# A macaron transformer layer on one core: causal masks moved from TensorE to VectorE and GpSimd, and the attention values issued two steps behind the scores

## The chip, the core and the metric

The kernel runs on one core of one Trainium2 chip, as one launch. The metric is the device time of that launch in microseconds; the kernel before was timed three times and the median counts. The core has five engines that run side by side and wait for each other through semaphores: TensorE (PE in the profile; PEld are its weight loads), VectorE (DVE), ScalarE (ACT), GpSimd (POOL) and SyncE (SP), whose queue issues most of the DMAs. Each engine executes its own instructions strictly in the order in which the program lists them, apart from weight loads that run ahead. Matmuls write to PSUM, which here is divided into eight banks of 128 partitions by 512 fp32 values.

## What is computed

The input is one sequence of 2048 tokens with 512 features. Three half-steps follow each other: a gated feed-forward network, causal self-attention with 16 heads of 32 features, and the same feed-forward network again, each on a layer-normed input and added to the residual.

```python
x = x + 0.5 * ffn(layernorm(x), gate, up, down)      # codes of 4 bits with block scales
x = x + attention(layernorm(x), w_qkv, b_qkv, w_out, b_out)
x = x + 0.5 * ffn(layernorm(x), gate, up, down)

def attention(x, w_qkv, b_qkv, w_out, b_out):
    q, k, v = split_heads(x @ w_qkv.T + b_qkv)        # 16 heads x 2048 x 32
    scores = q @ k.T / sqrt(32)
    scores = scores + triu(-inf, k=1)                 # causal
    return merge_heads(softmax(scores) @ v) @ w_out.T + b_out

def ffn(x, gate, up, down):
    return (gelu_tanh(x @ gate.T) * (x @ up.T)) @ down.T
```

The change touches the attention alone, and in it the causal mask, which affects only the 128x128 blocks on the diagonal of the score matrix: blocks above the diagonal are never computed.

## The kernel before

The whole kernel is written with an order by hand: the engines receive their instructions in the order in which the Python code issues them. Tiles come from pools with a fixed number of buffers; a tile's first writer waits for the last reader of the buffer's previous tile. Two PSUM pools matter: `ps_one` has seven banks and serves almost everything, and `ps_acc` has one bank, for the attention output being accumulated (`av`).

The attention works on eight pairs of heads, `p` = 0 to 7. Every pair is gone through twice:

- `maxima(p)` computes scores with queries on the partitions (tile `pm`, L612), and takes row maxima on VectorE (L629, tile `parts`). At the end of each block of 512 queries `g` (there are four), `finish` negates the maximum (L635, `nmax`), GpSimd splits it into three bf16 pieces (L640 and L643, five small instructions that depend on one another), and three steps later `rows` transposes them on TensorE (L650) and ScalarE copies them into `mrow` (L651).
- `attend(p)` computes the scores with keys on the partitions (tile `ps`): first a matmul with ones that puts minus the row maximum into the bank (L705, called `maxrows`), then keys times queries on top of it (L714). ScalarE exponentiates into an SBUF tile `pt` (L736; three buffers). `values` multiplies `pt` with the values and a block of ones, and so accumulates both the output and the softmax's denominator in `av` (L668).

Both run over the same 40 steps of a pair: for each `g` first 4g steps that lie below the diagonal and are 512 wide, then four diagonal steps of width 512, 384, 256 and 128. The main loop interleaves them: one step of `attend(p)` together with one step of `maxima(p + 1)`. The maxima of pair 0 run alone at the start, and pair 7 has no maxima beside it. One step issues, in this order: `maxrows` and the `pm` matmul for both heads, the `ps` matmuls for both heads, the mask matmuls of both sides, the maxima on VectorE (and `finish`), then the exponentials and `values` of the step before, which `pending` holds. A matmul here has 32 rows of contraction, and the two heads of pair p and the two of pair p+1 lie on the four different quarters of the array.

The mask is added by TensorE: on a diagonal step, `mask` issues eight bf16 matmuls for each side (L622 for `pm`, L726 for `ps`), of 32 rows, which add rows of a mask (`mqk`, `mkq`; -1e30 where a key is later than the query) picked by slices of an identity (`pick`). These three constant tiles are filled at the very start by 48 small DMAs on GpSimd's queue (L84).

Beside that run `fill` pieces, on the diagonal steps of some pairs: projections of q, k and v for later pairs (L540, L557; pairs 0, 2 and 4), and output projections (L579; pairs 3, 5 and 7). Pairs 1 and 6 have none, and the pieces of pairs 0 and 2 all fall on the first two diagonal steps. The wide tile of q and k weights for pair 2 is loaded by a DMA that is issued when pair 2 begins (L535).

When an `av` block is complete, ScalarE copies it (L677, `both`), two DMAs move the denominators to the partitions of the outputs (L682, `den`), and four chunks follow, one a step: a reciprocal on VectorE (L685) and two multiplications on GpSimd (L688). At the end of a pair the last `values` is issued at once, and `run_later(1 << 30)` issues at once the `rows` that are due later.

Of the kernel before, what the change touches and what calls it, by code (L numbers as in the profile page):

```python
# [18 lines left out]
P = 128  # L19
# [3 lines left out]
HD = 32  # L23
# [11 lines left out]
def macaron_kernel(ctx: ExitStack, tc: tile.TileContext, x, packed, scales, wqk, bqk, wv, bv, wo, bo, out):  # L35
# [34 lines left out]

    plain = [identb]
    for nm, step, mult in (("mask_qk", -1, 1), ("mask_kq", 1, -1)):
        m = const.tile([P, P], BF16, tag=nm, name=nm)
        nc.gpsimd.memset(m, 0.0)
        nc.gpsimd.affine_select(
            out=m, in_=m, compare_op=ALU.is_ge, fill=MASKED, base=0, pattern=[[step, P]], channel_multiplier=mult
        )
        plain.append(m)

    pick, mqk, mkq = [const.tile([P, 4, P], BF16, tag=nm, name=nm) for nm in ("pick", "mqk", "mkq")]  # L80
    for t4, src in zip((pick, mqk, mkq), plain):
        for r in range(4):
            for j in range(4):
                nc.gpsimd.dma_start(out=t4[HD * r : HD * r + HD, j, :], in_=src[HD * j : HD * j + HD, :])  # L84

# [403 lines left out]
    def attention(xT, xT_f):  # L489
        with tc.tile_pool(name="aw", bufs=1) as aw, tc.tile_pool(name="qk", bufs=1) as qkp, tc.tile_pool(  # L490
# [95 lines left out]
            def quadrant(p, a):  # L586
                r = 2 * (p % 2) + a
                return slice(HD * r, HD * r + HD)

            later, divisions = [], []  # L590

            def run_later(now):
                while later and later[0][0] <= now:
                    later.pop(0)[1]()

            def maxima(p):
# [5 lines left out]
                for g in range(NB):  # L602
                    parts = an.tile([P, 2, 4, g + 1], F32, tag=f"parts{g}", name=f"parts_{p}_{g}")
                    steps = [(i, kb) for i in range(4) for kb in range(g)] + [(i, g) for i in (3, 2, 1, 0)]
                    for i, kb in steps:
                        n = 512 if kb < g else (i + 1) * P
                        ps = [None, None]

                        def matmuls(a):
                            r = quadrant(p, a)  # L610
                            ps[a] = ps_one.tile([P, 512], F32, tag="one", name=f"pm_{p}_{g}_{i}_{kb}_{a}")
                            nc.tensor.matmul(  # L612
                                ps[a][:, :n], lhsT=q[r, bass.ts(4 * g + i, P)], rhs=k[r, kb * 512 : kb * 512 + n],
                                start=True, stop=(kb < g),
                            )

                        def mask():
                            if kb == g:
                                for j in (3, 2, 1, 0):
                                    for a in range(2):  # L620
                                        r = quadrant(p, a)
                                        nc.tensor.matmul(  # L622
                                            ps[a][:, n - P + HD * j : n], lhsT=pick[r, j, :], rhs=mqk[r, j, HD * j :],
                                            start=False, stop=(j == 0),
                                        )

                        def rest(now):
                            for a in range(2):
                                nc.vector.tensor_reduce(parts[:, a, i, kb : kb + 1], ps[a][:, :n], AX.X, ALU.max)  # L629
                            if i == 0 and kb == g:  # L630
                                finish(now)
# [27 lines left out]
            def attend(p):  # L659
# [5 lines left out]

                def values(g, c, off, pt, av):
                    for a in range(2):
# [7 lines left out]
                    if c == 4 * g + 3:  # L675
# [16 lines left out]

                        divisions.extend([lambda: None] * 2 + [lambda j=j: chunk(j) for j in range(4)])

                pending = None
                for g in range(NB):
                    av = None
                    for c in range(4 * g + 4):
# [13 lines left out]
                        def matmuls(a):  # L712
                            r = quadrant(p, a)
                            nc.tensor.matmul(  # L714
                                ps[a][:, off:],
                                lhsT=k[r, bass.ts(c, P)],
                                rhs=q[r, g * 512 + off : (g + 1) * 512],
                                start=False, stop=(c < 4 * g),
                            )

                        def mask():
                            if c >= 4 * g:
                                for j in range(4):
                                    for a in range(2):
                                        r = quadrant(p, a)
                                        nc.tensor.matmul(  # L726
                                            ps[a][:, off : off + HD * j + HD], lhsT=pick[r, j, :],
                                            rhs=mkq[r, j, : HD * j + HD],
                                            start=False, stop=(j == 3),
                                        )  # L730

                        def rest():
                            nonlocal pending, av
                            pt = pp.tile([P, 2, 512], F32, tag="pt", name=f"pt_{p}_{g}_{c}")
                            for a in range(2):
                                nc.scalar.activation(  # L736
                                    pt[:, a, off:], ps[a][:, off:], AF.Exp, scale=1.0 / math.sqrt(HD)
                                )
                            if pending is not None:
                                values(*pending)  # L740
                            if c == 0:
                                av = ps_acc.tile([P, 512], F32, tag="acc", name=f"av_{p}_{g}")
                            pending = (g, c, off, pt, av)

                        yield maxrows, matmuls, mask, rest, c >= 4 * g
                values(*pending)

# [12 lines left out]

            def after_step(diagonal, fill):

                nonlocal now
                now += 1
                run_later(now)
                if divisions:
                    divisions.pop(0)()
                if diagonal:
                    for _ in range(-(-len(fill[0]) // fill[1])):
                        fill[0].pop(0)()  # L770
                    fill[1] -= 1
# [21 lines left out]
            assert not fill  # L793
            run_later(1 << 30)
            plan = {
# [6 lines left out]
            for p in range(NPAIR):  # L802
# [18 lines left out]
                ahead = maxima(p + 1) if p + 1 < NPAIR else iter(())  # L821
                for n, (maxrows, matmuls, mask, rest, diagonal) in enumerate(attend(p)):
                    if n in STARTS:
# [10 lines left out]
                    if other:  # L834
                        other[1]()
                    mask()
                    if other:
                        other[2](now)
                    rest()
                    after_step(diagonal, fill)  # L840
                    for step in extra.get(n, ()):
                        step()
                run_later(1 << 30)
            while divisions:
                divisions.pop(0)()
            for piece in o3[12:]:
# [79 lines left out]
```

## The time and the profile before

| Kernel before | us |
|---|---|
| median of three runs | 3375.31 (3374.28 to 3377.02) |
| the profiled execution, its own time | 3374.09 |
| its span in the profile | 3372.3 |

The three stages, by windows of the trace (busy time of each engine in us, and the mean clock granted to TensorE as a share of full speed):

| Stage | window | PE | DVE | ACT | POOL | clock |
|---|---|---|---|---|---|---|
| first feed-forward | 0 to 1225 | 1178.60 | 922.26 | 214.69 | 661.82 | 0.99 |
| pair 0's maxima and the projections they need | 1225 to 1327 | 100.91 | 54.03 | 17.69 | 7.03 | 0.98 |
| pairs 0 to 7 | 1327 to 2180 | 836.1 | 492.9 | 358.7 | 161.7 | 0.97 to 1.00 |
| second feed-forward | 2180 to 3372 | 1167.87 | 598.48 | 203.51 | 303.30 | 0.99 |

(The third row adds up eight windows, cut at 1430, 1530, 1630, 1738, 1875, 1970 and 2070.) The cuts lie near the beginnings of pairs 1 to 7. The device time of the profiled execution is 1.8 us more than its span. A busy TensorE means that a matmul was in the array, not that all of it was in use: most matmuls in the attention occupy a quarter or a half of the array and run side by side, so what a step costs is read from the distance between its beginning and the next one's.

### The profile page before, as it was taken

The page shows a single profiled execution, that of the slowest core. Times are in us where ns is not written, and L with a number is a line of the kernel's source. Part 1 is how long each engine was busy: PE and PEld are TensorE (multiplying, and loading weights), DVE is VectorE, ACT ScalarE, POOL GpSimd, SP SyncE. Part 2 cuts the span into 40 slices and gives each one's busy share as a digit, 9 for nine tenths or more (in the row PEclk, how much of TensorE's full clock was granted, in tenths as well). Part 3 has the DMA queues.
Part 4 walks back from the last instruction along what each step waited for, and adds up shares of the span by engine and source line. Part 5 has one row for each costly group of instructions (what it writes and reads, how often), then busy time and mean ns, then how long its engine had stood idle before and what let it go on. Part 6 is the DMA issues. An engine that isn't in the chain of part 4 may idle for free.

```text
span 3372.3 us, 37369 instructions
## 1 busy us (share of the span) xinstructions
PE 3283.5 (97%) x14656; PEld 1772.4 (53%) x14656; DVE 2067.7 (61%) x3018; ACT 794.6 (24%) x1446; POOL 1133.8 (34%) x1258
## 2 busy tenths in 40 slices
PE   5999999999999989999999999899999999999998
PEld 3556565655656555333344333346565565656556
DVE  7887777877778555565655674445545454544545
ACT  2111111111111121443433444321111111111111
POOL 5455464554637331321111121012231222313223
PEclk8999999999999999999999999999999999999999
DMA  3111111111111010000000000010110101011101
GB/s 108 72 66 66 66 44 66 66 47 66 63 66 50 39 38 7 6 8 12 8 10 6 6 7 7 21 70 22 44 44 22 66 22 44 22 44 44 44 22 50
DMA packets 39488, 133.35 MB, mean 40 GB/s; under 512 B 4752, under 2 KB 21904, under 8 KB 32912
## 3 DMA queue, kind: packets, MB, share of 16 engines
q1 hardware_dynamic: 37776, 130.57, 10.6%
q8 instruction: 115, 1.88, 0.2%
q0 software_dynamic: 1536, 0.40, 0.1%
q14 instruction: 61, 0.50, 0.0%
HBM read 78.12 MB, written 48.23 MB: 37 GB/s over the span
## 4 chain that ended last, share of the span: by engine, by line
PE 95%; DVE 3%; ACT 1%; issue 1%; POOL 0%; DMA 0%; SPq 0%; POOLq 0%; ACTq 0%; DVEq 0%
PE po L366 23%; PE pu L271 22%; PE pg L271 22%; PE av L668 8%; PE pm L612 6%; PE pqk L540 4%; PE ps L705 3%; PE ps L714 2%; PE pp L579 2%; PE pv L557 2%; PE pt_f L122 1%; PE ps L726 0%; PE pm L622 0%; DVE st_f L95 0%; PE row L650 0%
## 5 line engine op out<-in xcount | busy, mean ns | idle before, releaser
L629 DVE TENSOR_REDUCE parts<-pm 128x1 f32<-128x512 f32 (+3 forms) x640 | 358.5, 604 | 213.7 <-PE ps L726 112.9
L271 PE MATMUL pg<-xT_f,w 128*128 128x512 f32 x1024 | 479.9, 597 | 9.1 <-DVE st_f L95 7.7
L366 PE MATMUL po<-wd,inter 128*128 128x256 f32 x2048 | 484.1, 381 | 0.0
L271 PE MATMUL pu<-xT_f,w 128*128 128x512 f32 x1024 | 475.9, 593 | 0.0
L366 PEld LDWEIGHTS po<-wd,inter 128*128 128x128 f32 x2048 | 391.1, 191 | 154.4 <-issue 104.9
L377 POOL TENSOR_TENSOR x<-x,d 128x512 f32<-128x512 f32 x256 | 340.5, 1341 | 351.6 <-DVE d L374 174.9
L323 POOL TENSOR_TENSOR u<-u,u 128x512 f32<-128x512 f32 x128 | 163.4, 1276 | 850.0 <-ACT u L320 841.7
L736 ACT ACTIVATE pt<-ps 128x512 f32<-128x512 f32 (+3 forms) x640 | 306.3, 531 | 416.2 <-PE ps L726 209.8
L366 PE MATMUL po<-wd,s 128*128 128x256 f32 x1536 | 362.2, 380 | 0.0
L271 PE MATMUL pg<-xsum,w 128*128 128x512 f32 x768 | 356.6, 594 | 0.0
L271 PE MATMUL pu<-xsum,w 128*128 128x512 f32 x768 | 355.4, 593 | 0.0
L366 PEld LDWEIGHTS po<-wd,s 128*128 128x128 f32 x1536 | 292.4, 191 | 115.5 <-issue 79.4
L612 PE MATMUL pm<-kT,qT 32*128 32x512 f32 (+3 forms) x1280 | 328.5, 575 | 0.1
L668 PE MATMUL av<-pt,vaug 128*64 128x512 f32 (+3 forms) x1280 | 305.9, 554 | 1.7 <-ACT pt L736 1.3
L271 PEld LDWEIGHTS pg<-xT_f,w 128*128 128x128 f32 x1024 | 196.3, 192 | 204.7 <-issue 187.7
L271 PEld LDWEIGHTS pu<-xT_f,w 128*128 128x128 f32 x1024 | 195.0, 191 | 193.3 <-issue 182.5
L714 PE MATMUL ps<-qT,kT 32*128 32x512 f32 (+3 forms) x1280 | 293.7, 533 | 0.0
L688 POOL TENSOR_TENSOR attnT<-both,den 32x128 f32<-32x128 f32 x256 | 115.3, 450 | 402.7 <-DVE den L685 321.6
L271 PEld LDWEIGHTS pu<-xsum,w 128*128 128x128 f32 x768 | 146.3, 191 | 144.9 <-issue 138.0
L271 PEld LDWEIGHTS pg<-xsum,w 128*128 128x128 f32 x768 | 146.3, 191 | 142.4 <-issue 133.9
L374 DVE SCALAR_TENSOR_TENSOR x<-po,x 128x512 f32<-128x512 f32 x192 | 131.5, 685 | 117.6 <-ACT d L381 84.9
L374 DVE SCALAR_TENSOR_TENSOR d<-po,d 128x512 f32<-128x512 f32 x192 | 131.7, 686 | 82.1 <-PE po L366 80.8
(128 smaller groups left out, 3575.2 us busy)
## 6 DMA issues: line engine op xcount, KB each, us to landing
kept<-wd SPq DMA_DIRECT2D x8, 1792.0 KB
wd<-kept SPq DMA_DIRECT2D x8, 1792.0 KB
x<-in_x SPq DMA_DIRECT2D x16, 256.0 KB
pk<-in_gate_codes SPq DMA_DIRECT2D x16, 256.0 KB
sc<-in_gate_scales SPq DMA_DIRECT2D x32, 128.0 KB
pk<-in_up_codes SPq DMA_DIRECT2D x16, 256.0 KB
sc<-in_up_scales SPq DMA_DIRECT2D x32, 128.0 KB
pk<-in_down_codes SPq DMA_DIRECT2D x16, 256.0 KB
```

Of the source, the lines that this page charges most:

```text
L271: nc.tensor.matmul(ps, lhsT=a[:, j, :], rhs=b[:, j, :], start=(j == 0), stop=(j == 1))
L323: nc.gpsimd.tensor_tensor(u4, u4, u2, ALU.add)
L366: nc.tensor.matmul(ps[:, j, :], lhsT=a[i][:, k, bass.ts(2 * q + j, P)], rhs=b[i][:, k, :], start=(k == 0), stop=(k == 1),)
L374: stt(dst, ps, 0.5, other, ALU.mult, ALU.add)
L377: nc.gpsimd.tensor_tensor(dst, dst, other, ALU.add)
L540: nc.tensor.matmul(ps, lhsT=w[:, j, k, :], rhs=xT[tb][:, k, :], start=(k == 0), stop=(k == 3))
L612: nc.tensor.matmul(ps[a][:, :n], lhsT=q[r, bass.ts(4 * g + i, P)], rhs=k[r, kb * 512 : kb * 512 + n], start=True, stop=(kb < g),)
L629: nc.vector.tensor_reduce(parts[:, a, i, kb : kb + 1], ps[a][:, :n], AX.X, ALU.max)
L668: nc.tensor.matmul(av[64 * a : 64 * a + 64, off:], lhsT=vaug[:, c, p % 4, HD * a : HD * a + 2 * HD], rhs=pt[:, a, off:], start=(c == 0), s ...
L688: nc.gpsimd.tensor_tensor(dst[quadrant(p, a), bass.ts(4 * g + j, P)], both[v, bass.ts(j, P)], rc[v, bass.ts(j, P)], ALU.mult,)
L714: nc.tensor.matmul(ps[a][:, off:], lhsT=k[r, bass.ts(c, P)], rhs=q[r, g * 512 + off : (g + 1) * 512], start=False, stop=(c < 4 * g),)
L736: nc.scalar.activation(pt[:, a, off:], ps[a][:, off:], AF.Exp, scale=1.0 / math.sqrt(HD))
```

## The change

- The mask matmuls go, and with them the constants `pick`, `mqk` and `mkq` and the 48 DMAs. One 128x128 mask is kept, in fp32 and in bf16.
- On the maxima's side VectorE adds the mask to the diagonal 128x128 part of the `pm` bank, in place, ahead of each reduction (two additions a diagonal step). Only for pair 0, whose maxima run alone, TensorE still adds it, by one full 128x128 bf16 matmul for each head.
- On the attention's side ScalarE copies the diagonal 128x128 part of both heads' scores unexponentiated into `pt`, GpSimd fills the masked part with -1e30 there (`affine_select` on 128x2x128), the rest of the width is exponentiated as before, and then ScalarE exponentiates the diagonal part in place, in one instruction for both heads.
- `values` runs two steps behind the scores instead of one, and what is pending is carried over the end of a pair; so are the `rows` that are due later.
- The chunks of the divisions are held back on diagonal steps as long as there are maxima beside them.

In the order that the program gives GpSimd, on the last diagonal step of a block `finish`'s five instructions stand ahead of that step's `affine_select`.

```diff
-    plain = [identb]
-    for nm, step, mult in (("mask_qk", -1, 1), ("mask_kq", 1, -1)):
...
-    pick, mqk, mkq = [const.tile([P, 4, P], BF16, tag=nm, name=nm) for nm in ("pick", "mqk", "mkq")]
-    for t4, src in zip((pick, mqk, mkq), plain):
-        for r in range(4):
-            for j in range(4):
-                nc.gpsimd.dma_start(out=t4[HD * r : HD * r + HD, j, :], in_=src[HD * j : HD * j + HD, :])
+    mask_f = const.tile([P, P], F32, tag="mask_f", name="mask_f")
...
+    nc.gpsimd.tensor_copy(mask_b, mask_f)
...
                         def mask():
-                            if kb == g:
-                                for j in (3, 2, 1, 0):
-                                    for a in range(2):
...
+                            if on_pe:
+                                for a in range(2):
+                                    nc.tensor.matmul(ps[a][:, n - P : n], lhsT=identb, rhs=mask_b, start=False, stop=True)
 
                         def rest(now):
                             for a in range(2):
+                                if kb == g and not on_pe:
+                                    own = ps[a][:, n - P : n]
+                                    nc.vector.tensor_tensor(own, own, mask_f, ALU.add)
                                 nc.vector.tensor_reduce(parts[:, a, i, kb : kb + 1], ps[a][:, :n], AX.X, ALU.max)
...
+                        def rest():
+                            pt = pp.tile([P, 2, 512], F32, tag="pt", name=f"pt_{p}_{g}_{c}")
+                            scale = 1.0 / math.sqrt(HD)
+                            plain = off
                             if c >= 4 * g:
...
+                                plain = off + P
+                                own = pt[:, :, off:plain]
+                                for a in range(2):
+                                    nc.scalar.copy(own[:, a], ps[a][:, off:plain])
+                                nc.gpsimd.affine_select(
+                                    out=own, in_=own, compare_op=ALU.is_ge, fill=MASKED, base=0,
+                                    pattern=[[0, 2], [1, P]], channel_multiplier=-1,
                                 )
-                            if pending is not None:
-                                values(*pending)
...
+                            if plain < 512:
+                                for a in range(2):
+                                    nc.scalar.activation(pt[:, a, plain:], ps[a][:, plain:], AF.Exp, scale=scale)
+                            if plain > off:
+                                nc.scalar.activation(own, own, AF.Exp, scale=scale)
+                            pending.append(lambda args=(g, c, off, pt): values(*args))
+                            if len(pending) > 2:
+                                pending.pop(0)()
...
-                values(*pending)
...
-                if divisions:
-                    divisions.pop(0)()
+                if divisions and not (divisions[0] and diagonal and masks):
+                    step = divisions.pop(0)
+                    if step:
+                        step()
...
-                run_later(1 << 30)
-            while divisions:
-                divisions.pop(0)()
+            assert not later
+            while pending:
+                pending.pop(0)()
+            for step in divisions:
+                if step:
+                    step()
```

## The prediction

> **What bounds the kernel now.** I read the chain that ended last first, then the stage windows, then the timeline of a pair without fill pieces (pair 1), the waits, and the pair ends.
>
> ```profile
> PE 95%; DVE 3%; ACT 1%; issue 1%; POOL 0%; DMA 0%; SPq 0%; POOLq 0%; ACTq 0%; DVEq 0%
> ...
> 1430.00:1530.00 100.00, 95.79 (x972) 37.24 (x970) 63.53 (x110) 47.53 (x99) 19.66 (x57) 1.00 0.05 12
> ...
> 1457.24 0.39 PE L705 MATMUL ps<-mrow,ones_b 3*128 3x512 bf16 x1
> 1458.42 1.08 PE L668 MATMUL av<-pt,vaug 128*64 128x512 f32 x4
> 1459.43 0.39 PE L705 MATMUL ps<-mrow,ones_b 3*128 3x512 bf16 x1
> 1460.77 1.08 PE L668 MATMUL av<-pt,vaug 128*64 128x512 f32 x4
> 1461.78 0.33 PE L705 MATMUL ps<-mrow,ones_b 3*128 3x384 bf16 x1
> ...
> 1345.45 0.49 DVE L629 TENSOR_REDUCE parts<-pm 128x1 f32<-128x128 f32 x2 [0.64 <-PE ps L726]
> 1346.04 0.16 DVE L635 TENSOR_REDUCE nmax<-parts 128x8 f32<-128x8 f32 x1
> 1346.34 0.22 POOL L640 CAST split<-nmax 128x8 bf16<-128x8 f32 x1 [11.64 <-DVE nmax L635]
> 1347.47 0.22 POOL L640 CAST split<-left 128x8 bf16<-128x8 f32 x1
> ...
> 1329.89 0.63 PE L650 MATMUL row<-identb,split 128*64 128x128 bf16 x4 [2.87 <-POOL split L640]
> 1339.54 3.70 PE L540 MATMUL pqk<-xT_a,wqk 128*128 128x512 f32 x8
> 1526.41 0.41 PE L650 MATMUL row<-identb,split 128*64 128x128 bf16 x4 [1.12 <-POOL split L640]
> 1531.30 6.05 PE L540 MATMUL pqk<-xT_a,wqk 128*128 128x512 f32 x8 [3.13 <-DMA wqk<-in_wqk]
> ...
> 31.54 1.44 POOL L230 TENSOR_TENSOR w<-w 128x256 f32<-128x256 f32 x1
> 32.33 0.94 DVE L191 TENSOR_SCALAR mag<-pk 128x512 uint32<-128x512 uint32 x1
> ```
>
> TensorE is on 95% of the chain. In the window of pair 1 it is busy for 95.8 of 100 us and no other engine for over 64. A plain step lasts 2.19 us (1457.24 to 1459.43), of which the scores take 1.18 and the values 1.01. The diagonal step of the same width lasts 2.35: its scores take 1.34. So the masks of both sides cost 0.16 us a step, though each matmul is listed with about 0.2 us: they overlap. The next lines show the end of a query block: VectorE's maximum at 1346.04, then GpSimd's split until 1347.69. The last lines show stalls at pair ends: 2.87 us ahead of pair 0, 1.12 and 3.13 at the beginning of pair 2, and behind the 3.13 eight projection matmuls that take 6.05 instead of 3.70.
>
> **What the Trainium skill says.** "TensorE: Matmul & The Clock Gate", section "What's actually happening": after an idle window of some 3.4 us TensorE runs at half clock until it has been busy for as long. The trace agrees: the slow matmuls follow just these two stalls, none follows one of 1.1 us. "ScalarE: Activation LUTs", section "What ACT_TABLE_LOAD costs": an activation takes 186 ns plus 0.833 ns an element, and neighbours overlap by about 93 ns; the trace has 275, 381 and 595 ns for 128, 256 and 512. So cutting an exponential in two costs a fixed part again. "VectorE: DVE Perf Modes", section "The DRAIN you can't avoid": reading what the previous VectorE instruction wrote needs a semaphore. The changed program waits so between each addition and its reduction; the gap from `parts` to `nmax` suggests 0.08 to 0.1 us. "GPSIMD Engine Reference", section "3.1 Elementwise — side-by-side cycle accounting": GpSimd pays more for two inputs than for one; here additions of 128x256 take 0.72 to 0.84 us and `affine_select` on 128x128 takes 0.29.
>
> **The sum.** It is made against the profiled execution (3374.1 us, span 3372.3), which lies 1.2 us under the median.
>
> *Masks off TensorE.* 112 steps (7 pairs x 16) lose both sides: 112 x 0.155 = 17.4. Pair 7's 16 steps lose one side; its filled diagonal step of 3.40 against 2.19 plus the 1.06 of an output projection shows 0.15 too: 2.4. Pair 0's maxima keep two full-array matmuls for eight small ones; I take 1. Together **-20.8**. TensorE is the bound there, so this counts in full unless something else comes late.
>
> *What comes late on unfilled diagonal steps.* VectorE gets two additions a step. There is no row for 128x128; 0.691 at 512 (L582) and 0.419 at 256 (L565) give 0.28, with 0.08 for the wait. Bounds: 0.25, and 0.45. With reductions of 0.69, 0.55, 0.42 and 0.28 a head, its four steps need 2.1, 1.8, 1.55 and 1.3, against TensorE's 2.2, 2.0, 1.7 and 1.25: VectorE just keeps up, and `nmax` is there 2.1 us after the last diagonal step began (before: 1.4). ScalarE needs 1.75, 1.5 and 1.5 us for two copies (0.45), the rest and the diagonal part (0.38); that is inside the steps too, and two-step values do not need `pt` sooner. `affine_select` on 128x256: 0.29 at 128, plus a slope like that of memsets (0.204 at 128, 0.524 at 512) gives 0.40; bounds 0.29 and 0.84, the addition.
>
> On the last step of a block, time 0 at its beginning: GpSimd's queue has the split first, 2.1 + 0.14 + 1.35 = 3.6, then the fill of `pt`, 4.05; ScalarE exponentiates the diagonal part until 4.58. Behind that blocked instruction in ScalarE's queue stand the next step's two exponentials (1.08), one more pair, and `both` (0.59). TensorE would start its next steps at 1.22 and 2.98. It wants those values at 4.16 and gets them at 4.65, 0.49 late. After them and `rows` (0.59 together) it needs the banks that the next step's exponentials free at 5.66: 5.72 instead of 5.24, 0.48 late. Its first values of the new block wait for `both`, 5.66 + 1.08 + 0.59: 7.4 instead of 6.9, 0.50 late. That is 1.47; before, `both` alone cost 0.24 here (values at 1348.93, scores done 1.18 after 1347.51). So +1.23 a block end, in the 12 inside pairs 0, 1, 2 and 6: **+14.8**. Pairs 3, 4 and 5 have fill pieces of 1.06 us or more behind the last diagonal step, which hide it: 0.
>
> *Pair ends.* Ahead of pair 0, 2.87 goes, and with it the slow clock: the first step takes 7.0, where its like takes 5.98, less 1.01 for values it has not got, so 2.0 more: -4.9; `rows` comes at step 3, under fills. Pair 1 to 2: the values' and `rows`' stall (1.4), the DMA's 3.13 and the slow clock's 2.4 go: -6.9. The load moves ahead of the last block's two `den` DMAs in SP's queue, which wait for `both`; its own tile has been free since pair 0. Pair 2 to 3, 3 to 4 and 6 to 7: stalls of 1.4, 0.4 and 1.4 go, and `both`, now behind two diagonal steps' activations on ScalarE, costs 0.55, 0 and 0.8: -1.85. Pair 4 to 5: 0. Pair 0 to 1 and 5 to 6 have no cover: stalls of 2.4 and 1.3 go (steps of 3.36 and 2.94 against 1.85 and 2.08), but the same queue on ScalarE makes the third step's scores 0.75 and its values 1.6 late on top of the 0.5: 2.9 and 1.8, +1.0. Together **-12.7**.
>
> *The start.* Without 48 DMA issues (POOL until 31.5) the first weight sums run at 18 instead of 31.5, beside VectorE's statistics and not beside its decoding on the chain, whose four instructions take 0.94, 1.09, 0.83 and 0.94 there against 0.42, 0.69, 0.43 and 0.42 alone; the sums before them lose 0.4: **-2.2**.
>
> *The end of pair 7.* All values run ahead of the last `den` wait, in another order; 0. Held chunks of a pair are done by step 7 of the next, ahead of the output projections that read them; 0.
>
> Sum: -20.8 + 14.8 - 12.7 - 2.2 = -20.9, 3353.2 for this execution, **3354** on the median.
>
> **Rivals.** *A, the forecast*, 3346 to 3364: 0.58. *B, the block ends cost nothing new*: if VectorE's additions cost 0.25 without a gap and GpSimd is quick, the split ends earlier and the 14.8 goes: 3339. For it: VectorE is 64% busy; against: the split alone took until 2.9 us after its step began, even before. 0.14. *C, VectorE becomes the bound of diagonal steps*: at 0.45 an addition its four steps need 1 us more than TensorE's 7.1, and block ends cost double: +15.8, about 3370; a variant is that the mask matmuls were free anyway, against which the 0.16 speaks. 0.17, half of it within 0.2% (6.7 us, about what a measurement can tell). *D, slower: ScalarE blocked by GpSimd.* In-order ScalarE stands still while GpSimd splits and fills. Everything else gains 36.7; the 14 uncovered ends (12 and two pair ends) cost 15.8 of it. The point is 2.6 us an end; that needs the diagonal exponential at 6.0 instead of 4.6 after the step's beginning, as when GpSimd takes 1.8 for its fill. At 3.3 us an end: +46.2 - 36.7, 3385. For it: five dependent GpSimd instructions stand in front; against: 0.29 at 128 wide. 0.11.
>
> Faster: A, B and half of C, 0.80; same 0.09; slower 0.11. The range 3340 to 3371 holds A, over half of B and most of C.
>
> **What would show it.** Diagonal steps of pair 1 at 2.2, 2.0, 1.7 and 1.25 us; no idle time ahead of the first `row` of pair 0 and the first projection of pair 2; TensorE idle for about 1.5 us in the two to three steps behind each unfilled block end, put down to ScalarE; `affine_select` of 0.4 us behind the split. It is wrong if plain steps leave 2.19, if VectorE ends the waits on diagonal steps, or if GpSimd's fill takes a microsecond or more.

## The result and the profile after

| Kernel | median us | runs | its profiled execution | span |
|---|---|---|---|---|
| before | 3375.11 (3374.28 to 3377.02) | 4 | 3374.09 | 3372.3 |
| after | 3351.74 (3347.49 to 3353.61) | 4 | 3353.61 | 3351.8 |

The ratio is 0.9928, with a 95% interval from 0.9911 to 0.9945: the changed kernel is 23.4 us faster by the medians, and 20.5 us faster in the two profiled executions, between which the traces are compared. (The lines have moved: in the new program `maxrows` is L702, `pm` L610, `ps` L711, `values` L667, the reduction L625, the split L636 and L639, `rows` L646 and L647, `both` L676, the reciprocal L684, `affine_select` L728, the exponentials L734 and, for the diagonal part, L736.)

First the chain that ended last, from the page of the changed kernel:

```profile
PE 96%; DVE 3%; ACT 1%; issue 0%; POOL 0%; DMA 0%; SPq 0%; POOLq 0%; ACTq 0%; DVEq 0%
```

TensorE is still the bound. Then a window of 100 us from the end of pair 0 to the beginning of pair 2 (busy time of PE, PEld, DVE, ACT and POOL, clock, DMA share, GB/s):

```profile
1420.00:1520.00 100.00, 99.33 (x676) 32.96 (x676) 76.92 (x154) 55.30 (x149) 26.52 (x74) 1.00 0.04 12
```

The window counts some 300 matmuls less than its like did before (676 for 972), yet TensorE is listed as busy for 99.3 us instead of 95.8. The records of neighbouring matmuls overlap and their ends are modelled, so the busy time says little here; what a step costs is the distance from its beginning to the next one's. The timeline of TensorE in pair 1 shows plain steps and the first diagonal one:

```profile
1451.50 0.39 PE L702 MATMUL ps<-mrow,ones_b 3*128 3x512 bf16 x1
...
1452.68 1.08 PE L667 MATMUL av<-pt,vaug 128*64 128x512 f32 x4
1453.69 0.39 PE L702 MATMUL ps<-mrow,ones_b 3*128 3x512 bf16 x1
...
1454.88 1.08 PE L667 MATMUL av<-pt,vaug 128*64 128x512 f32 x4
1455.89 0.33 PE L702 MATMUL ps<-mrow,ones_b 3*128 3x384 bf16 x1
```

The plain step takes 2.19 us (1451.50 to 1453.69), as before, and the diagonal step of full width 2.20 (1453.69 to 1455.89) instead of 2.35: the 0.155 us for masks is gone. The pair ends are smooth as well; in the timeline of the changed kernel neither the first `row` of pair 0 nor the first projection of pair 2 has idle time ahead of it:

```profile
1334.34 0.41 PE L646 MATMUL row<-identb,split 128*64 128x128 bf16 x4
...
1520.45 1.98 PE L533 MATMUL pqk<-xT_a,wqk 128*128 128x512 f32 x4
```

What came late shows only when all steps of a block are laid side by side. These are distances between the beginnings of steps in block 1 of pair 1 (us), four diagonal steps and the three behind the block end:

| | diagonal | | | | behind | | | sum |
|---|---|---|---|---|---|---|---|---|
| before | 2.35 | 2.08 | 1.61 | 1.18 | 1.55 | 2.65 | 2.20 | 13.62 |
| after | 2.19 | 1.94 | 1.66 | 1.24 | 1.77 | 1.79 | 3.01 | 13.60 |

Over such a block nothing is gained. Of 4 x 0.155 = 0.62 us for the masks all but 0.02 is given back, and the place is the third step behind the block end, 3.01 us against 2.19 for a plain one. It is so in pairs with fill pieces too (pair 3: 17.84 before, 17.83 after, third step 3.02). What the kernel won inside the attention lies at the pair ends. In the timeline of the kernel before, that third step begins at 1470.86 and the next at 1473.06:

```profile
1470.86 0.39 PE L705 MATMUL ps<-mrow,ones_b 3*128 3x512 bf16 x1
...
1473.06 0.39 PE L705 MATMUL ps<-mrow,ones_b 3*128 3x512 bf16 x1
```

In the changed kernel it lasts from 1464.29 to 1467.30. Its timeline there:

```profile
1461.50 0.22 POOL L636 CAST split<-nmax 128x8 bf16<-128x8 f32 x1 [1.93 <-DVE nmax L631]
...
1462.79 0.41 POOL L728 TENSOR_SCALAR_AFFINE_SELECT pt<-pt 128x256 f32<-128x256 f32 x1
1463.09 0.94 DVE L684 RECIPROCAL den<-den 128x128 f32<-128x128 f32 x1
1463.23 0.42 ACT L736 ACTIVATE pt<-pt 128x256 f32<-128x256 f32 x1 [2.67 <-POOL pt L728]
1463.55 2.04 ACT L734 ACTIVATE pt<-ps 128x512 f32<-128x512 f32 x4
...
1463.95 1.22 DVE L625 TENSOR_REDUCE parts<-pm 128x1 f32<-128x512 f32 x2
...
1464.29 0.39 PE L702 MATMUL ps<-mrow,ones_b 3*128 3x512 bf16 x1
...
1464.67 0.18 PEld L610 LDWEIGHTS pm<-kT,qT 32*128 32x128 f32 x1 [0.30 <-ACT pt L734]
...
1465.22 0.18 PEld L610 LDWEIGHTS pm<-kT,qT 32*128 32x128 f32 x1 [0.26 <-DVE parts L625]
...
1465.46 0.61 ACT L676 COPY both<-av 128x512 f32<-128x512 f32 x1
...
1466.29 0.20 PEld L667 LDWEIGHTS av<-pt,vaug 128*64 128x64 f32 x4 [0.76 <-ACT both L676]
...
1467.30 0.38 PE L702 MATMUL ps<-mrow,ones_b 3*128 3x512 bf16 x1
```

Two engines are late at once. ScalarE stood for 2.67 us behind `affine_select`, which stood behind the split; four exponentials follow, and TensorE's first `pm` waits for one of them. VectorE had a reciprocal ahead of the second step's reductions, and the second `pm` waits for these until 1465.22. Which of the two sets the time, the trace alone does not say.

### The profile page after: what moved, and what is told of

Same layout as the page of the kernel before. It is cut to its first block, busy times and chain, and to the rows that moved or that the text cites. A ratio compares the mean times of both kernels' runs of the same rounds, so it can differ in the third digit from the quotient of the medians.

```text
span 3351.8 us, 34007 instructions
## 1 busy us (share of the span) xinstructions
PE 3276.4 (98%) x12640; PEld 1734.2 (52%) x12640; DVE 2128.5 (64%) x3242; ACT 848.4 (25%) x1766; POOL 1157.9 (35%) x1337
## 4 chain that ended last, share of the span: by engine, by line
PE 96%; DVE 3%; ACT 1%; issue 0%; POOL 0%; DMA 0%; SPq 0%; POOLq 0%; ACTq 0%; DVEq 0%
PE po L359 23%; PE pu L264 23%; PE pg L264 23%; PE av L667 8%; PE pm L610 6%; PE pqk L533 4%; PE ps L702 3%; PE ps L711 2%; PE pp L572 2%; PE pv L550 2%; PE pt_f L115 1%; DVE st_f L88 0%; PE pt_a L115 0%; DVE parts L625 0%; PE row L646 0%
## 5 line engine op out<-in xcount | busy, mean ns | idle before, releaser
L625 DVE TENSOR_REDUCE parts<-pm 128x1 f32<-128x512 f32 (+3 forms) x640 | 367.3, 604 | 92.9 <-PE pm L610 81.6
L610 PE MATMUL pm<-kT,qT 32*128 32x512 f32 (+3 forms) x1280 | 338.1, 574 | 0.5 <-DVE parts L625 0.4
L734 ACT ACTIVATE pt<-ps 128x512 f32<-128x512 f32 (+3 forms) x576 | 271.8, 531 | 149.6 <-PE ps L711 148.9
L667 PE MATMUL av<-pt,vaug 128*64 128x512 f32 (+3 forms) x1280 | 304.2, 554 | 0.8 <-ACT both L676 0.6
L711 PE MATMUL ps<-qT,kT 32*128 32x512 f32 (+3 forms) x1280 | 292.9, 531 | 0.0
```

The costliest lines, as they stand in the source:

```text
L610: nc.tensor.matmul(ps[a][:, :n], lhsT=q[r, bass.ts(4 * g + i, P)], rhs=k[r, kb * 512 : kb * 512 + n], start=True, stop=not on_pe,)
L667: nc.tensor.matmul(av[64 * a : 64 * a + 64, off:], lhsT=vaug[:, c, p % 4, HD * a : HD * a + 2 * HD], rhs=pt[:, a, off:], start=(c == 0), s ...
L711: nc.tensor.matmul(ps[a][:, off:], lhsT=k[r, bass.ts(c, P)], rhs=q[r, g * 512 + off : (g + 1) * 512], start=False, stop=True,)
L734: nc.scalar.activation(pt[:, a, plain:], ps[a][:, plain:], AF.Exp, scale=scale)
```

## The experiments

Ratios are against the kernel before on the same chip. Runs are numbered 1 to 12 as they were made. "Unfilled" are pairs 0, 1, 2 and 6, which have no fill pieces on the last two diagonal steps of a block, "filled" pairs 3, 4 and 5.

### Runs 1 and 2: the carry over pair ends, alone and left out

The first run takes the kernel before and only carries `values` (still one step behind) and `rows` over pair ends; the second takes the changed kernel and issues both at once at a pair's end, as before.

```diff
 # run 1, on the kernel before
-                            if pending is not None:
-                                values(*pending)
...
+                            pending.append(lambda args=(g, c, off, pt): values(*args))
+                            if len(pending) > 1:
+                                pending.pop(0)()
...
-                values(*pending)
...
-            run_later(1 << 30)
 # run 2, on the changed kernel, at a pair's end
+                while pending:
+                    pending.pop(0)()
...
+                run_later(1 << 30)
```

> Kernel before with one edit: the pending values (still one step behind) and the rows that are due are carried over pair ends; masks stay on TensorE, the mask DMAs stay. Theory 1 (the gain comes from pair ends and the start, the masks give nothing net inside a pair): all stalls at pair ends go, and ScalarE adds none, 4.9 + 2.4 + 6.9 + 1.4 + 0.4 + 1.3 + 1.4 = 18.7 less, about 3356; the block steps stay 2.35, 2.08, 1.61, 1.18, 1.55, 2.65, 2.2. Rival (the masks off TensorE are the gain, the carry is a few us): 3368 or more.

> Kernel after with one part undone: values and rows are issued at once at every pair end, as before. Theory 1: the stalls at the pair ends come back, about 15 to 18 us, 3367 to 3370; first step of pair 0 about 7 again, a DMA wait of about 3 us at the beginning of pair 2. Rival (masks are the gain): at most 6 us more, 3358.

Run 1: 3362.96 us, ratio 0.9962 [0.9949, 0.9975]. Run 2: 3383.29 us, 1.0022 [1.0015, 1.0029]. So the carry alone brings 13 us (3376.13 for the kernel before in that set, less 3362.96) of the 18.7 expected, and without it the changed kernel is 7 us slower than before. The parts do not add: in the changed kernel the carry is worth about 31 us, twice what I expected. The last step of a pair shows why. It takes 3.3 us before, 1.2 with the carry, and 4.75 in run 2. The timeline of run 2 at the end of pair 0:

```profile
1442.57 0.20 PEld L667 LDWEIGHTS av<-pt,vaug 128*64 128x64 f32 x4 [2.87 <-ACT pt L736]
```

The mask's new way from ScalarE over GpSimd and back is a long latency, and issuing the last values at once exposes all of it. Part of the 31 us is the clock: in the trace of run 2, 30.7 us of the pairs ran at half the clock, behind waits at the pair ends (granted clock 0.98 on average from 1330 to 2180, and 0.74 from 1440 to 1460), in that of the changed kernel none (1.00 from 1330 to 2150). That costs up to half of the 30.7, 15 us, as an estimate.

### Run 3: values one step behind the scores

```diff
-                            if len(pending) > 2:
+                            if len(pending) > 1:
```

> Kernel after with the values one step behind instead of two. If the lag covers ScalarE's wait for GpSimd at block ends: the values of the last diagonal step are wanted about 2.4 us after it begins and come at 3.9 to 4.6, so 1 to 2 us more at each of some 25 block ends, about 3377. Rival (the lag does nothing, as plain steps have no stall): 3352.

3395.51 us, ratio 1.0057 [1.0041, 1.0074]: 44 us more than the changed kernel. The first two steps behind a block end take 3.31 and 3.55 us in unfilled pairs and 2.62 and 2.41 in filled ones, against 1.77 and 1.80. The second step of distance pays for itself by hiding the same latency inside the pairs. I had expected 25 us, not 44. The clock has a part in the rest: 34.1 us of the pairs ran at half the clock here (0.98 on average from 1330 to 2190), which by the same estimate costs up to 17 us.

### Run 4: the split behind the fill

```diff
-                                finish(now)
+                                ended.append(lambda: finish(now))     # issued after rest(), so behind affine_select
```

> Kernel after with GpSimd's split (and nmax) issued behind that step's affine_select instead of ahead of it. Theory A of the long third step behind a block end (3.01 us instead of 2.19): ScalarE stands blocked behind the split; then the step falls to about 2.4 and the kernel by 27 x 0.6 = 13 to 16 us, 3337. Theory B: TensorE waits there for a bank that VectorE's reduction frees, late because a reciprocal of a held-back chunk stands ahead of it; then the step stays at 2.9 to 3.0 and the time at 3350.

3352.02 us, ratio 0.9928 [0.9914, 0.9943]; the third step stays at 3.01. ScalarE is no longer late, and TensorE waits for VectorE instead, as the timeline of this run shows:

```profile
1464.85 0.18 PEld L610 LDWEIGHTS pm<-kT,qT 32*128 32x128 f32 x1 [0.65 <-DVE parts L625]
```

By this run alone ScalarE's queue looked innocent; a later one takes that back.

### Runs 5 and 7: the reciprocal left out, or held one step more

The first kernel drops the reciprocals; the second keeps them and holds the chunks on the first step behind a block end too, with a third buffer for `both` and `den`.

```diff
 # run 5
-                            nc.vector.reciprocal(rc[:, bass.ts(j, P)], rc[:, bass.ts(j, P)])
 # run 7
-                if divisions and not (divisions[0] and diagonal and masks):
+                if divisions and not (divisions[0] and (diagonal or behind) and masks):
```

> Kernel after without the reciprocals of the denominators on VectorE (left out: the output is multiplied by the denominator instead of divided by it). Theory B1 (the third step behind a block end waits for a bank that a reduction frees, and the reduction is late because a reciprocal of 0.94 us stands ahead of it in VectorE's queue): the third step falls from 3.01 to 2.4 to 2.6. Theory B2 (the bank wait is there without the reciprocal, since two short steps leave VectorE no time for its reductions alone): it stays at 2.9 or more.

> Kernel after with the chunks of the divisions held back for one more step, the first behind a block end (three buffers instead of two for what waits). Theory B1: the reductions of the next step begin 0.7 us earlier, the third step falls to about 2.5, 21 x 0.5 = 10 us, 3342. Theory B2: no change, 3352.

Without reciprocals 3348.25 us in one run, and a third step of 2.84 (unfilled) and 2.79 (filled). Held: 3345.88 us, ratio 0.9911 [0.9895, 0.9928], with the same two steps. So the reciprocal's place costs 0.2 us at each block end, which holding recovers in full, but 0.6 over a plain step is left.

### Run 6: the rows two steps later

`rows` comes five steps behind the maxima instead of three, so that it no longer lies just ahead of the third step.

```diff
-                            later.append((now + 3, rows))
+                            later.append((now + (8 if g == NB - 1 else 5), rows))
```

> Kernel after with the transposed maxima (rows) issued five steps after a block end instead of three (eight at a pair's last block). The rows take one of the seven banks, and so the third step waits for the second reduction of the step before instead of the first. If that is the wait: the third step falls to 2.2 to 2.5, some 0.5 us at 21 block ends, 0.2 of it given back where the rows now stand: about 3343. If the reductions are late whatever bank is waited for: 2.8 or more and 3350.

3348.79 us, ratio 0.9916 [0.9902, 0.9931]. Its transposes (0.22 us) move from the second step (1.79 to 1.58) to the fourth (2.19 to 2.42). The third step is 2.64 in filled pairs, but 3.07 in unfilled ones.

### Runs 9 to 12: combinations

Split behind the fill with chunks held; split behind the fill without reciprocals; all three edits; chunks held and rows later, with the split in its old place.

> The changed kernel with both edits at once: VectorE's additions for the split and -max issued behind GpSimd's fill (so that ScalarE's exponentials of the step before do not queue behind the split's copies), and the chunks of the division held one step more behind a block end (so that VectorE's reductions do not queue behind a reciprocal). Theory 'two covers' (each of the two waits ends late enough to hide the other, so each edit alone gives 0.0 and 0.2 us): the third step behind a block end falls from 3.01 us to 2.2 to 2.5, that is 0.5 to 0.8 us at each of 21 block ends, and the time to 3335 to 3343 us. Theory 'one cover' (VectorE alone; ScalarE's exponential is late by the copies of the sums that it makes for the division, which neither edit moves): the step stays at 2.8, the time at 3344 to 3350.

> The changed kernel with VectorE's additions for the split and -max behind GpSimd's fill, and without the reciprocals on VectorE (the output is then multiplied by the denominators instead of divided by them). Nothing of the division is moved, only one of its operations is gone. 'Two covers': the third step behind a block end is 2.2 to 2.5 us, time 3335 to 3345. 'One cover' (what is left is ScalarE's copy of the sums): it stays at 2.8 as without the reciprocals alone, 3346 to 3352.

> As the run with both edits, and the rows of -max of a block issued five steps behind its maxima instead of three (eight at the last block of a pair), so that they do not fall into the third step. 'Two covers': 2 to 4 us below the run with both edits, as the rows' move alone gave about 3 us against the changed kernel. If the rows' move only shifts a wait: within 1.5 us of it.

> The changed kernel with the chunks of the division held one step more behind a block end and the rows of -max issued five steps behind the maxima (eight at the last block of a pair), but with VectorE's additions for the split back in front of GpSimd's fill. Each of the two edits alone left a long third step (2.84 and 3.06 us; it is 3.01 in the changed kernel), all three edits together left 2.41. Theory 'two waits on VectorE, one behind the reciprocal and one because the row takes a PSUM bank between the scores' banks': the order at the fill plays no part, the third step is 2.4 to 2.5 and the time within 1.5 us of the run with all three. Theory 'ScalarE's queue behind the split counts once the others are gone': the third step is 2.6 to 2.8, the time 3342 to 3347.

The third step behind the inner block ends (median), and the times:

| Changed kernel with | unfilled | filled | us | ratio |
|---|---|---|---|---|
| nothing else | 3.01 | 3.02 | 3351.74 | 0.9928 [0.9911, 0.9945] |
| split behind the fill | 3.01 | 3.02 | 3352.02 | 0.9928 [0.9914, 0.9943] |
| chunks held | 2.84 | 2.79 | 3345.88 | 0.9911 [0.9895, 0.9928] |
| rows later | 3.07 | 2.64 | 3348.79 | 0.9916 [0.9902, 0.9931] |
| split, held | 2.78 | 2.79 | 3345.45 | 0.9913 [0.9896, 0.9929] |
| split, no reciprocals | 2.78 | 2.79 | 3344.86 (one run) | |
| held, rows later | 3.06 | 2.41 | 3346.51 | 0.9914 [0.9900, 0.9927] |
| split, held, rows later | 2.41 | 2.41 | 3338.15 | 0.9892 [0.9877, 0.9907] |

Several of these expectations fell. Runs 5, 6 and 7 ended between their two theories, and run 11 came 7.3 us below run 9 where I had put 2 to 4. After the first two combinations I had ruled out that the split's order matters: the step stayed at 2.78, as the theory of a single cover said, though what covers it was not ScalarE's copy of the sums, as I had written. The last run then showed the split's order to be worth 0.65 us at every unfilled block end, once the other two are out of the way. Each step in the table is the later of two limits. VectorE's is there at every block end: 3.02 us as changed (less where no reciprocal stands ahead: the first block end of pair 0 takes 2.84, and 2.79 with the split moved), 2.79 with the chunks held, 2.64 with the rows moved, 2.41 with both; the column of the filled pairs shows it alone. ScalarE's is there in the unfilled pairs only, and goes with the split's order: 2.84 us with the rows in their place (the row with held chunks), 3.06 with the rows moved, since the second step, in which ScalarE catches up, is then 0.22 shorter. The later of the two gives every other entry of the first column within 0.01 us. In the changed kernel ScalarE's 2.84 hides under VectorE's 3.02, which is why moving the split alone did nothing; and removing VectorE's causes alone brings ScalarE's up.

VectorE's limit, in the timeline of the run with split and chunks both moved, whose third step begins at 1462.37:

```profile
1461.74 1.29 DVE L625 TENSOR_REDUCE parts<-pm 128x1 f32<-128x512 f32 x2 [0.48 <-PE pm L610]
...
1461.94 0.33 PEld L646 LDWEIGHTS <-split 128*64 128x64 bf16 x4
...
1463.08 0.18 PEld L610 LDWEIGHTS pm<-kT,qT 32*128 32x128 f32 x1 [0.42 <-DVE parts L625]
```

Even with no reciprocal ahead of them, the second step's reductions end at 1463.03, and the third step's second `pm` begins only then. With the rows moved as well (third step from 1462.16), the same reductions end even later against the step's beginning (0.87 us behind it instead of 0.66), and no `pm` waits for them:

```profile
1461.74 1.29 DVE L625 TENSOR_REDUCE parts<-pm 128x1 f32<-128x512 f32 x2 [0.48 <-PE pm L610]
...
1462.60 0.18 PEld L610 LDWEIGHTS pm<-kT,qT 32*128 32x128 f32 x1
...
1462.89 0.59 ACT L676 COPY both<-av 128x512 f32<-128x512 f32 x1
...
1463.55 0.20 PEld L667 LDWEIGHTS av<-pt,vaug 128*64 128x64 f32 x4 [0.76 <-ACT both L676]
```

That the row's transposes make a `pm` wait for VectorE is shown; that they do so because the row takes one of the seven banks of `ps_one`, so that the next tiles get younger banks, is the reading that fits, and was not tried by itself. The 0.22 us left over 2.19 is the wait for `both`, which was 0.24 in the kernel before.

ScalarE's limit, in the timeline of the run with chunks held and rows later, whose third step begins at 1460.85:

```profile
1459.57 0.41 POOL L728 TENSOR_SCALAR_AFFINE_SELECT pt<-pt 128x256 f32<-128x256 f32 x1
1460.01 0.42 ACT L736 ACTIVATE pt<-pt 128x256 f32<-128x256 f32 x1 [2.67 <-POOL pt L728]
1460.33 2.04 ACT L734 ACTIVATE pt<-ps 128x512 f32<-128x512 f32 x4
...
1462.24 0.61 ACT L676 COPY both<-av 128x512 f32<-128x512 f32 x1
...
1462.90 0.20 PEld L667 LDWEIGHTS av<-pt,vaug 128*64 128x64 f32 x4 [1.05 <-ACT both L676]
```

ScalarE waits 2.67 us for the fill, then works without a gap through four exponentials to `both` at 1462.85, and only then the new block's first values start. In run 11 `both` ended 1.32 us after the third step's beginning; here it is 2.00, and the step is 0.65 longer.

The version with all three edits is 13.6 us faster than the changed kernel by the medians (12 by the ratios, as the two were timed in different sets) and 36 us faster than the one before in its set (3374.33).

### Run 8: the constants' DMAs alone

The kernel before, with its 48 mask DMAs issued eight at a time during the first feed-forward network instead of at the start.

```diff
-                nc.gpsimd.dma_start(out=t4[HD * r : HD * r + HD, j, :], in_=src[HD * j : HD * j + HD, :])
+                mask_dmas.append(lambda t4=t4, src=src, r=r, j=j: nc.gpsimd.dma_start(...))
...
+                for _ in range(min(8 if g > 0 else 0, len(mask_dmas))):
+                    mask_dmas.pop(0)()
```

> Kernel before with the 48 mask DMAs issued in groups of eight during the first feed-forward network instead of at its start. If the start gains because the first weight sums on GpSimd no longer run beside VectorE's decoding: the first full run of matmuls begins 2.4 us earlier (at 88.8 instead of 91.2), and the kernel is about 2 us faster, 3374, if the later issues cost nothing. Rival (the difference at the start is chance, or comes from the DMAs' traffic): no change there.

3375.37 us over 20 runs, ratio 0.9994 [0.9987, 1.0000]. The timeline of this run, at the decoding that the prediction showed with 0.94 us for a like instruction:

```profile
32.31 0.42 DVE L196 TENSOR_SCALAR mag<-pk 128x512 uint32<-128x512 uint32 x1
32.77 0.69 DVE L197 SCALAR_TENSOR_TENSOR mag<-pk,mag 128x512 uint32<-128x512 uint32 x1
33.49 0.43 DVE L198 TENSOR_SCALAR mag<-mag 128x512 uint32<-128x512 uint32 x1
33.84 0.42 DVE L199 TENSOR_SCALAR val<-pk 128x512 uint32<-128x512 uint32 x1
```

The decoding is undisturbed, and the first long run of up-projections begins at 88.62 instead of 91.19 us. The mechanism is there; 2.2 us in the total agrees with the interval, which reaches from no gain to 4.4 us. Other runs with an undisturbed decoding began that run of matmuls anywhere from 88.6 to 91.7, so one start does not prove the size.

## Why the prediction was right, and where its steps were not

The forecast of -20.9 us met -20.5 in the traces and -23.4 in the medians. That it came so close is luck: the sum hides errors that cancel. Inside pairs 0 to 7 the trace gained 21.5 us (from the first step of pair 0 to the first matmul of the second feed-forward network), where the terms of the sum put 14.8 there; outside it lost 1.0 instead of gaining 6.1.

| Term | predicted | measured |
|---|---|---|
| masks off TensorE in pairs 0 to 6 | -17.4 | -17.4: 0.155 to 0.16 a step |
| pair 7, with its end | -2.4 | -2.6, by luck |
| block ends | +14.8 = 12 x 1.23 | about +12.6 = 21 x 0.60 |
| pair ends, without the 2.87 ahead of pair 0 | -9.8 | -14.1, what is left of the 21.5 |
| ahead of pair 0, with its maxima | -3.9 | -2.2 |
| the start | -2.2 | -2.35 |
| slow clock elsewhere | 0 | +5.5 |

*Masks.* Right inside the pairs, and so was the forecast that VectorE keeps up on diagonal steps: they take 2.19, 1.94, 1.66 and 1.24 where I had 2.2, 2.0, 1.7 and 1.25. The estimates of new instructions held: addition 0.29 us (0.28), `affine_select` 0.41 (0.40), diagonal exponential 0.42 (0.38). Pair 7 met its figure by luck. One of its steps in the last block took 5.06 us before and takes 3.25 after: the kernel before waited there for exponentials that stood behind two loads of function tables on ScalarE (1.28 us each, for a square root at L102 and back at L736), and two-step values cover that wait. I had not seen this 1.8 us. Another 1.9 us are lost behind the pair's last step, in part because more values are left to do there.

*Block ends.* Right in the sum, wrong in place and in part in cause. "Pairs 3, 4 and 5 have fill pieces [...] which hide it: 0" is the sentence that failed: all 21 inner block ends of pairs 0 to 6 lose 0.6. ScalarE's queue behind the split does what I described, and only where I put it, but costs 0.43 to 0.65 (2.84 against the 2.41 without either limit, and 3.06 against 2.41 with the rows moved) instead of 1.23. In run 12 the fill ends 3.71 us after the last diagonal step began and the diagonal exponential 4.16, where I had 4.05 and 4.58. So the first of my three delays, 0.49 for the values of that step, all but vanished: TensorE starts them at 4.21, and by my count wants them at 4.16. And a second limit, VectorE's reductions, is there at every end and in most cases later still (3.02 against 2.84). Of that I had nothing in the sum. I had priced neither the held chunks, which put a reciprocal ahead of the second step's reductions, nor the row's transposes, beside which the two-step distance makes a `pm` wait. I followed a single engine's queue to the end, found a limit, and did not ask what else falls on the same step.

*Pair ends.* The stalls went as listed (pair 1 to 2: 7.3 us net of masks, for 6.9). The new waits for `both` that I set against them at the ends 2 to 3, 3 to 4 and 6 to 7 (1.35) did not come: together these ends gave about 3.8 for 1.85. The ends 0 to 1 and 5 to 6, at which I had a loss of 1.0, gained 0.2 together. The first step of pair 0 gave 2.0, as forecast. Its second is 0.8 shorter too, but mostly because its values come a step later, and that is paid back at the end of pair 7. Run 1 shows 13 us for the carry by itself.

*Outside.* The 5.5 us come from the clock, behind two waits of 2.90 us that both kernels have; the last section shows on what that depends. The 1.7 missing ahead of pair 0 was not followed further.

*The rivals.* Rival C falls with the diagonal steps' lengths and D with 0.41 us for the fill, though the wait that D names exists. B, block ends that cost nothing, put the time at 3339; the kernel in which these waits are taken out measures 3338.15, so B's price for the block ends was close (13.6 against 14.8), though in places where I had none, and its reason (a quick split) was not what it took. That the two times agree within 1 us is luck, since the other terms are off by more.

## What to carry to other kernels

When a mask or any small step is moved from the bottleneck engine to a chain over two others, its latency has to be hidden everywhere, at the ends of loops most of all: the same change is worth -23 us with the pipeline carried over pair ends and +7 without. When one step of a loop is long, list everything that is late on it before trying edits: with two limits of nearly the same length one edit alone shows little, and can clear a suspect that is guilty. Spread what falls behind a block end (copies, reciprocals, transposes) over different steps.

## What the runs showed of the hardware

Whether a wait slowed TensorE's clock depended on where it fell, not on its length alone. Near the end of the first feed-forward network TensorE waits 2.90 us for a layer norm, in both kernels. TensorE's timeline of the kernel before:

```profile
1213.04 0.72 PE L122 MATMUL pt_a<-ident,xn_a 128*128 128x128 f32 x4 [2.90 <-DVE xn_a L114]
1213.60 1.89 PE L366 MATMUL po<-wd,s 128*128 128x256 f32 x8
```

and of the changed one:

```profile
1210.67 1.10 PE L115 MATMUL pt_a<-ident,xn_a 128*128 128x128 f32 x4 [2.90 <-DVE xn_a L107]
1211.56 3.62 PE L359 MATMUL po<-wd,s 128*128 128x256 f32 x8
```

The same wait, the same eight matmuls, 1.89 and 3.62 us; the clock granted in 10 us around them is 1.00 and 0.67. The slow form came in seven of the fourteen traces (the changed kernel, runs 2 to 5, 10 and 11) and not in the others (before, runs 1, 6 to 9 and 12); the changed kernel and runs 6, 7, 9 and 12 do not differ in that part of the program. It happened to the changed kernel a second time, ahead of its second feed-forward network, behind a wait of 2.90 us as well.

What differs is the place of the wait on a grid of time. In all fourteen traces the granted clock is either full or half, and it changes only at points that lie a whole multiple of 3.41 us apart. These points cut the span into stretches of 3.41 us. The two waits of 2.90 us make 28 cases. In 15 of them TensorE had no matmul in the array for 59 to 85% of one stretch, and it ran at half clock in the next. In the other 13 a point of the grid split the wait so that no stretch was idle for more than 57%, and the clock stayed full. This holds for these two waits. Among the pairs, whose matmuls fill only part of the array, the clock also fell behind shorter idle times (2.42 us in run 2).

So the prediction read its two stalls (2.87 and 3.13 us) too simply. It said that they agree with an idle window of some 3.4 us, and that the slow matmuls follow just these two. Both stalls are shorter than 3.41, the wait of 2.90 in the same trace slowed nothing, and behind a wait of 1.95 us at 1197.66 eight matmuls like the above took 3.53 us (1.89 in run 11).

The price also varies. In the changed kernel each of the two cases costs about 2.8 us. In runs 2, 3 and 11 the slow clock behind the first of these waits cost 1.5 to 1.7 us against runs 7 and 9, but there the wait of 1.95 us was not followed by a slow clock, which gave as much back. Differences of 3 us between single runs of these kernels mean nothing.

VectorE's integer operations with one input, 0.42 us for 512 elements, took 0.83 to 0.94 us beside GpSimd's additions, and those with two inputs 1.09 instead of 0.69. Moving GpSimd's work away from them gave all of that back. It is the additions and not the mask DMAs that matter: after the first 100 us of the kernel before, where no mask DMA is left, 28 operations of one of these lines (L191) run beside GpSimd's additions and take 0.89 us (median). Eight of that line have no addition beside them, and take 0.42.
